# A copy that joins two 16-bit halves: which index runs innermost

## The chip, the cores and the metric

The kernel runs on one core of a Trainium2 chip. A core has a matrix engine (TensorE, PE in the profile, with its weight loads shown apart as PEld), a vector engine (VectorE, DVE), a scalar engine (ScalarE, ACT), GpSimd (POOL), and a queue for data transfers (SyncE, SP). They run beside one another and wait for one another by semaphores. Data lie in SBUF; TensorE writes its results into PSUM, and VectorE and ScalarE read them from there. Both memories have 128 partitions. The metric is the time of the whole program on the device in microseconds, as the median of several runs.

## The reference

Four graph-attention layers run over 16 graphs of 1024 nodes with 256 features. All share one 1024 x 1024 adjacency matrix. Each layer normalises its input and adds its output to it:

```python
h = jnp.maximum(_layernorm(x, axis=-1), 0.0)
x = x + layer(h, adj, W, a)
```

Layers 0, 1 and 3 (with 4, 1 and 4 heads) form `Wh = h @ W`, one score per node as source and one as destination, and mix the values with softmax weights:

```python
e = s_src[:, :, None, :] + s_dst[:, None, :, :]
e = jnp.where(e > 0, e, NEG_SLOPE * e)
alpha = jax.nn.softmax(jnp.where(mask, e, -jnp.inf), axis=2)
h_out = jnp.einsum('bijh,bjhd->bihd', alpha, Wh)
```

Layer 2 has one head, takes its scores from products of queries and keys (`h1 @ h2.T`) and ends in a relu instead of an elu.

## The kernel before, in words

**Tiling.** Rows of x are held in tiles of 128 nodes, eight to a graph (`NT`), and the 256 features in two chunks of 128 (`KC`). Attention works on halves of 512 query nodes.

**Order of work.** Every piece of work of all 64 pairs of graph and layer is a step with an engine, a planned cost and a due time (`Plan.add`). `Plan.order` plays the steps through with the planned costs and fixes one order for each engine; the instructions are then written in that order. Layers of neighbouring graphs overlap, so that TensorE has attention products of one layer while another layer is prepared. On the chip each engine goes through its list in order and waits where something isn't ready. The planned cost of the step that matters here is 0.95 (L920); it steers the order only.

**The prologue of a layer** (`Layer.prologue`, L827) turns normalised rows into values and scores. For each pair of row tiles it does this:
1. ScalarE normalises two tiles into `h` (`normed`, L883).
2. TensorE transposes them (`turned`, L897). A 32-bit transpose is done as two transposes of the two 16-bit halves of each number (`halves`, L587), each written into its own part of one PSUM tile `pp` of shape [128, side 2, chunk 2, 256 nodes] in 16-bit elements. A part holds 512 elements, 1 KB in each partition; the tile is 2 KB.
3. ScalarE copies the PSUM tile to SBUF and joins the halves to 32-bit numbers again (`kept`, L912 to L918). The target is `hTp` for layers 0, 1 and 3, and a slice of `hT` for layer 2. There are four such copies to a layer, 256 in the program.
4. TensorE multiplies the joined tile with the weights (`projected`, L925, by `product`, L569). The joined tile is the stationary operand, so its weight load is the instruction that waits for the copy.
5. ScalarE and VectorE bring the result to `val` and `ke` (L941 to L960).

A second place, `keep` at L1022 to L1024, joins halves in the same manner for the scores of a layer; the change leaves it alone. `pp` has four buffers, `hTp` two and `h` four; a buffer comes free when its last reader is done.

**The rest.** VectorE forms the attention weights `p` (L1089, L1179; L1211 and L1212 for layer 2) and TensorE multiplies them with `val` into `acc` and `accb`. L572 is the line of all of TensorE's products and L585 that of the transposes by halves.

Of the kernel before, what the change touches and what calls it, by code (L numbers as in the profile page):

```python
# [12 lines left out]
U16 = mybir.dt.uint16  # L13
# [516 lines left out]
def fast(  # L530
# [16 lines left out]
    nc = tc.nc  # L547
# [17 lines left out]
    def buf(tag, shape, dtype=F32, name=None):  # L565
        pool = psum if tag in ("pp", "acc", "accb") else sb
        return pool.tile(shape, dtype, name=name or tag, tag=tag, bufs=bufs[tag])

    def product(to, stationary, moving, start, stop):  # L569

        for c in range(0, P, COLS):
            nc.tensor.matmul(  # L572
                to[c : c + COLS],
                stationary[:, c : c + COLS],
                moving,
                start=start,
                stop=stop,
                skip_group_check=True,
            )
# [239 lines left out]
    class Layer:  # L819
# [7 lines left out]
        def prologue(self, due, step, stats, direct=False):  # L827
# [8 lines left out]
            T = {}  # L836
# [3 lines left out]
            for n, its in enumerate(parts):  # L840
# [30 lines left out]
                s = plan.add(DVE, 0.2, at, norm, (*stats[its], ready[-1] if n else None))  # L871
                s = plan.add(POOL, 2.0, at, norm2, (s,))
# [5 lines left out]
            for t0 in range(0, NT, run):  # L878
# [28 lines left out]
                s = plan.add(PE, 0.47 * n, at, turned, norms, take=("pp",) * n, give=("h", "h") * n)  # L907
                turns.update(dict.fromkeys(pairs, s))
            for n, t0 in enumerate(range(0, NT, 2)):
                at, s = due + n * step, turns[t0]  # L910

                def kept(t0=t0):  # L912
                    if self.gat:
                        T["hT", t0] = buf("hTp", [P, KC, 2 * P])
                    else:
                        T["hT", t0] = self.hT[:, :, t0 * P : (t0 + 2) * P]
                    bits = T["hT", t0].bitcast(U16).rearrange("p c (q s) -> p s c q", s=2)
                    nc.scalar.copy(bits, T["tp", t0].bitcast(U16))  # L918

                s = plan.add(ACT, 0.95, at, kept, (s,), take=("hTp",) if self.gat else (), give=("pp",))  # L920
                copies.append(s)
                for k in range(2):
                    t = t0 + k

                    def projected(t=t, t0=t0, k=k):  # L925
                        pv = T["pv", t] = buf("pp", [P, HALF])
                        for c in range(KC):
                            product(
                                pv[:, :cols],
                                T["hT", t0][:, c, k * P : (k + 1) * P],  # L930
                                w[:, c, :cols],
                                start=(c == 0),
                                stop=(c == KC - 1),
                            )

                    s2 = plan.add(
                        PE, 0.9, at + (k + 1) * step / 3, projected, (s, w_ready), take=("pp",),
                        give=("hTp",) if k and self.gat else (),
                    )

                    def evict(t=t):  # L941
                        to = self.val[:, t, :, :d]
                        of = T["pv", t][:, :F].rearrange("p (h d) -> p h d", h=heads)
                        if not self.gat:
                            nc.scalar.copy(to, of)
                            return
                        a = self.val[:, t, :, d : d + 1]

                        nc.scalar.activation(
                            a, T["pv", t][:, F + heads : cols].unsqueeze(2), AF.Exp, scale=1.0 / (SLOPE - 1.0)  # L950
                        )
                        nc.scalar.activation(self.ke[:, :, t], T["pv", t][:, F:cols], AF.Exp)
                        if heads == 1:
                            nc.scalar.mul(to, of, a[:, 0, :])

                    def scaled(t=t):
                        to = self.val[:, t, :, :d]
                        of = T["pv", t][:, :F].rearrange("p (h d) -> p h d", h=heads)
                        a = self.val[:, t, :, d : d + 1]
                        nc.vector.tensor_mul(to, of, a.to_broadcast([P, heads, d]))  # L960

                    many = heads > 1
                    cost = 0.4 if many or not self.gat else 0.8
                    s2 = plan.add(ACT, cost, at, evict, (s2,), give=() if many else ("pp",))
                    if many:
                        s2 = plan.add(DVE, 0.43, at, scaled, (s2,), give=("pp",))
                    evicted.append(s2)
            at = due + 4 * step
            self.ready, self.queries = evicted, ([], [])
            if not self.gat:  # L970
                for dc in range(KC):
                    for n0 in range(0, N, HALF):
# [12 lines left out]
                        s = plan.add(PE, 1.72, at, query, (*copies, *w12_ready), take=("pp",))  # L985
# [8 lines left out]
            if direct:  # L994
                for half in range(2):
                    for hd in range(heads):
# [7 lines left out]
                        def keep(half=half, hd=hd):  # L1004
# [3 lines left out]
                        s = plan.add(  # L1008
                            PE, 0.44, at + (half * heads + hd) * 0.01, spread, tuple(evicted[half * HT : (half + 1) * HT]),
                            take=("pp", f"row{heads}"), wide=True,  # L1010
                        )
# [19 lines left out]
            s = plan.add(PE, 0.14, at, factors, tuple(evicted), take=("pp",))  # L1031
            s = plan.add(ACT, 0.35, at, keep, (s,), give=("pp",))
            s = plan.add(SP, 0.1, at, store, (s,))
            stored = landed(s, at, 16)
            for half in range(2):
                for hd in range(heads):
# [6 lines left out]
                    s = plan.add(SP, 0.5, at + (half * heads + hd) * 0.01, load, (stored,), take=(f"row{heads}",))  # L1043
# [402 lines left out]
```

## Time and profile before

The time before is 3062.7 us (median of 3 runs, 3062.08 to 3062.9). The profiled run's span is 3059.6 us.

| engine | busy us | share |
|---|---|---|
| TensorE, products | 3017.0 | 99% |
| TensorE, weight loads | 2467.5 | 81% |
| VectorE | 2722.5 | 89% |
| ScalarE | 1524.6 | 50% |
| GpSimd | 127.6 | 4% |

How to read it: busy times of different engines overlap, so they don't add up to the span. A row of the profile names the line, the engine, the operation, the tile written and the tiles read, the shape, the count, the busy time with the mean of one instruction in ns, and then the idle time of the engine before these instructions with what ended it. The idle time of an engine that isn't the bottleneck costs nothing by itself. A line of the waits view gives who waited for whom, the sum in us, the number of waits and the longest.

### The profile page before, as it was taken

The numbers are of one execution on the slowest core, as the hardware profiler recorded it, in microseconds if no ns is written. First come the engines' busy times: TensorE is split into PE (matmuls) and PEld (weight loads), VectorE is DVE, ScalarE is ACT, GpSimd is POOL, SyncE is SP. The second block draws the span as 40 slices with busy tenths as digits, with TensorE's granted clock in tenths as the row PEclk, the third lists the DMA queues.
The fourth block names the chain that finished last, engine by engine and source line by source line (L and its number), as shares of the span: only waits on it lengthen the run. The fifth ranks groups of instructions, "written<-read, shape, count | busy, mean of one in ns | idle before, by whom it ended". The sixth has DMA issues, their size and how long they took to land.

```text
span 3059.6 us, 115063 instructions
## 1 busy us (share of the span) xinstructions
PE 3017.0 (99%) x52018; PEld 2467.5 (81%) x52018; DVE 2722.5 (89%) x5551; ACT 1524.6 (50%) x3352; POOL 127.6 (4%) x115
## 2 busy tenths in 40 slices
PE   7999999999999999999999999999999999999998
PEld 5887868778787887878788787887878878786876
DVE  8999969989889898998989989898998989986788
ACT  5573656544644446454454543546444464445443
POOL 1000000000000000000000000000000000000000
PEclk9999999999999999999999999999999999999999
DMA  3110003111010111101111011110111101010110
GB/s 127 51 51 23 27 16 99 37 40 48 20 60 23 37 54 26 58 23 35 49 37 51 19 41 47 37 51 16 55 33 37 55 23 44 23 30 26 30 33 24
DMA packets 82161, 123.41 MB, mean 40 GB/s; under 512 B 6976, under 2 KB 42496, under 8 KB 81664
## 3 DMA queue, kind: packets, MB, share of 16 engines
q1 hardware_dynamic: 81248, 115.47, 12.4%
q8 instruction: 409, 6.70, 0.9%
q14 instruction: 88, 0.72, 0.1%
q10 hardware_dynamic: 416, 0.52, 0.1%
HBM read 98.63 MB, written 17.33 MB: 38 GB/s over the span
## 4 chain that ended last, share of the span: by engine, by line
PE 94%; DVE 4%; ACT 1%; issue 0%; DMA 0%; SPq 0%; DVEq 0%; ACTq 0%
PE pp L572 33%; PE accb L572 29%; PE acc L572 29%; PE pp L585 3%; DVE p L1089 3%; ACT hT L918 0%; ACT hTp L918 0%; DVE bn L813 0%; DVE xt L1066 0%; DMA xt<-in_x_dram 0%; DVE o L1065 0%; DVE mv L814 0%; PE pp L1002 0%; PE tpm L585 0%; PE er L585 0%
## 5 line engine op out<-in xcount | busy, mean ns | idle before, releaser
L1089 DVE SCALAR_TENSOR_TENSOR p<-row,ke,mask 128x512 f32<-128x512 f32 x2048 | 1412.6, 743 | 55.3 <-PE acc L572 51.5
L572 PEld LDWEIGHTS acc<-val,p 128*64 128x64 f32 x32768 | 1066.8, 138 | 80.2 <-issue 37.1
L572 PE MATMUL acc<-val,p 128*64 128x65 f32 x32768 | 1080.9, 223 | 18.2 <-DVE p L1089 17.5
L572 PE MATMUL accb<-val,p 128*64 128x257 f32 x8192 | 928.6, 380 | 0.0
L572 PEld LDWEIGHTS accb<-val,p 128*64 128x64 f32 x8192 | 765.3, 137 | 103.6 <-issue 6.4
L572 PE MATMUL pp<-qT,hT 128*64 128x512 f32 x2048 | 457.7, 592 | 0.0
L572 PE MATMUL pp<-w,hTp 128*64 128x264 f32 (+1 forms) x3072 | 376.9, 386 | 1.3 <-ACT hTp L918 0.3
L572 PEld LDWEIGHTS pp<-qT,hT 128*64 128x64 f32 x2048 | 189.6, 137 | 205.9 <-issue 204.0
L572 PEld LDWEIGHTS pp<-w,hTp 128*64 128x64 f32 x3072 | 241.7, 137 | 81.0 <-ACT hTp L918 8.6
L1246 ACT ACTIVATE o<-accb,rdens 128x256 f32<-128x256 f32 x128 | 60.6, 474 | 470.9 <-DVE rdens L1238 432.9
L886 ACT ACTIVATE h<-xt,nshift,rstd 128x256 f32<-128x256 f32 x512 | 273.4, 600 | 12.7 <-DVE nshift L852 12.7
L918 ACT COPY hTp<-pp 128x1024 uint16<-128x1024 uint16 x192 | 248.8, 1324 | 54.9 <-PE pp L585 54.8
L1211 DVE SCALAR_TENSOR_TENSOR p<-u,p 128x512 f32<-128x512 f32 x256 | 175.6, 686 | 61.9 <-ACT p L1207 61.3
L1206 ACT ACTIVATE u<-pp 128x512 f32<-128x512 f32 x256 | 153.0, 598 | 150.8 <-PE pp L572 136.6
L813 DVE BATCH_NORM_STATS2 bn<-xt 128x6 f32<-128x256 f32 x512 | 212.3, 415 | 14.7 <-DMA xt<-in_x_dram 5.2
L1244 ACT ACTIVATE o<-accb,rden 128x256 f32<-128x256 f32 x128 | 60.6, 473 | 330.5 <-DVE rden L1238 330.5
L849 POOL TENSOR_TENSOR rstd<-rstd,neg_half 128x8 f32<-128x8 f32 (+1 forms) x66 | 117.9, 1786 | 2118.8 <-DVE rstd L846 1799.4
L1212 DVE TENSOR_TENSOR p<-p,mask 128x512 f32<-128x512 f32 x256 | 177.1, 692 | 8.8
L1179 DVE SCALAR_TENSOR_TENSOR p<-row,ke,mask 128x512 f32<-128x512 f32 x256 | 183.4, 739 | 0.0
L1207 ACT ACTIVATE p<-pp,shift_col 128x512 f32<-128x512 f32 x256 | 175.2, 684 | 0.0
L1060 ACT ACTIVATE ex<-o 128x1024 f32<-128x1024 f32 (+1 forms) x195 | 122.1, 626 | 90.2 <-DVE o L1133 85.8
L585 PEld LDWEIGHTS <-h 128*64 128x64 bf16 x4096 | 145.5, 111 | 24.0 <-issue 13.3
(84 smaller groups left out, 1912.4 us busy)
## 6 DMA issues: line engine op xcount, KB each, us to landing
row<-er_d SPq DMA_DIRECT2D x272, 256.0 KB
xt<-in_x_dram SPq DMA_DIRECT2D x32, 512.0 KB
out_dram<-xt SPq DMA_DIRECT2D x31, 512.0 KB
raw<-in_adj_dram SPq DMA_DIRECT2D x4, 1024.0 KB
raw<-in_adj_dram SPq DMA_DIRECT2D x16, 256.0 KB
w<-in_L_gnn_W_dram SPq DMA_DIRECT2D x2, 256.0 KB
wraw<-in_L_gnn_W_dram SPq DMA_DIRECT2D x2, 256.0 KB
er_d<-er_s SPq DMA_DIRECT2D x30, 16.0 KB
```

The costliest lines, as they stand in the source:

```text
L572: nc.tensor.matmul(to[c : c + COLS], stationary[:, c : c + COLS], moving, start=start, stop=stop, skip_group_check=True,)
L585: nc.tensor.transpose(to[c : c + COLS], of[:, c : c + COLS], ident_b)
L813: nc.vector.bn_stats(st, x_tiles[b][:, t, :])
L886: nc.scalar.activation(h, x_tiles[b][:, t, :], AF.Relu, bias=T["shift"][:, t : t + 1], scale=T["rstd"][:, t : t + 1],)
L918: nc.scalar.copy(bits, T["tp", t0].bitcast(U16))
L1060: nc.scalar.activation(ex, o, AF.Exp)
L1089: nc.vector.scalar_tensor_tensor(p, lay.rows[half, hd], lay.ke[:, lay.heads + hd, jt : jt + 1], mask_of(half, jt), op0=OP.max, op1=OP.mult)
L1179: nc.vector.scalar_tensor_tensor(p, lay.rows[half, 0], lay.ke[:, 1, jt : jt + 1], mask_of(half, jt), op0=OP.max, op1=OP.mult)
L1206: nc.scalar.activation(u, e, AF.Exp, scale=1.0 - SLOPE)
L1207: nc.scalar.activation(p, e, AF.Exp, bias=shift_col, scale=SLOPE)
L1211: nc.vector.scalar_tensor_tensor(p, u, 1.0, p, op0=OP.max, op1=OP.mult)
L1212: nc.vector.tensor_mul(p, p, mask_of(half, jt))
```

## The change

The copy runs through 1024 elements in each partition: two chunks c, 256 nodes q and two sides s. In SBUF the two sides of one number are neighbours, in PSUM they lie 512 elements apart. Before, the side is the outermost index: the copy reads PSUM in one contiguous run and writes every second 16-bit place, first all of one side and then all of the other. After it, the side is the innermost index: the copy writes SBUF in one contiguous run (for the slice of `hT`, one run for each chunk) and reads PSUM alternately from the two parts. It is for writing SBUF contiguously. The values, the number of instructions, the planned cost and the steps are the same.

```diff
-                    bits = T["hT", t0].bitcast(U16).rearrange("p c (q s) -> p s c q", s=2)
-                    nc.scalar.copy(bits, T["tp", t0].bitcast(U16))
+                    bits = T["hT", t0].bitcast(U16).rearrange("p c (q s) -> p c q s", s=2)
+                    nc.scalar.copy(bits, T["tp", t0].bitcast(U16).rearrange("p s c q -> p c q s"))
```

## The prediction

> **What bounds the kernel now.** I read the first parts of the page first: engine shares, then the chain that ended last.
>
> ```profile
> PE 3017.0 (99%) x52018; PEld 2467.5 (81%) x52018; DVE 2722.5 (89%) x5551; ACT 1524.6 (50%) x3352; POOL 127.6 (4%) x115
> ...
> PE 94%; DVE 4%; ACT 1%; issue 0%; DMA 0%; SPq 0%; DVEq 0%; ACTq 0%
> ```
>
> TensorE is busy for 99% of the span and is 94% of the chain; ScalarE, the engine of the changed instruction, is busy half of the time and makes 1% of the chain. So what the copy costs ScalarE is not yet a cost of the kernel. It becomes one where TensorE stands still for the copy. The order of all instructions is fixed when the program is built, from planned costs that the change leaves alone, so TensorE can't do other work instead: a wait there is lost for good, and a wait removed there is won.
>
> Next, the changed line and who waits for it, and TensorE's list of waits.
>
> ```profile
> L918 ACT COPY hTp<-pp x192: 1296/1321/1371, 14.5 to 2991.0; 128x1024 uint16<-128x1024 uint16 x192
> L918 ACT COPY hT<-pp x64: 1296/1331/1358, 174.2 to 2881.0; 128x1024 uint16<-128x1024 uint16 x64
> ...
>   PEld pp L572: 12.3, 55
>   PE pp L572: 0.3, 1
> ```
>
> ```profile
> PEld acc L572 <- DVE p L1089: 15.9, 18, 4.7
> ...
> PEld pp L572 <- ACT hTp L918: 8.6, 35, 0.6
> ...
> PEld pp L572 <- ACT hT L918: 3.7, 20, 0.2
> ```
>
> There are 192 + 64 = 256 copies of 1.32 us. TensorE stood still for 56 of them, 12.3 + 0.3 = 12.6 us in all, or 0.4% of the span. That is the ceiling of what a faster copy can win directly. One such wait, from the timeline:
>
> ```profile
> 717.10 1.11 PE L585 MATMUL pp<-ident_b,h 128*64 128x128 bf16 x32
> 717.81 2.50 ACT L918 COPY hTp<-pp 128x1024 uint16<-128x1024 uint16 x2 [0.34 <-PE pp L585]
> 717.94 0.68 PEld L572 LDWEIGHTS pp<-w2v,hT 128*64 128x64 f32 x8
> 719.17 0.86 PEld L572 LDWEIGHTS pp<-w,hTp 128*64 128x64 f32 x10 [0.56 <-ACT hTp L918]
> ```
>
> The transposes end, the copy starts at 717.81 and takes 1.32 us to 719.12, TensorE runs one other projection and then stands until 719.17, 50 ns after the copy. Here each ns on the copy is a ns on the kernel.
>
> How many copies are like this? I followed each of the 256 copies in the trace to the first weight load that reads its tile. The distance from the copy's end to that load is under 0.06 us for 66 copies, under 0.3 us for 99, under 0.6 us for 147 and under 1.0 us for 170; the other 86 have more. About 0.05 us is the handover itself. So the slack is short: the median is under 0.5 us.
>
> **What a copy element costs.** The rows by shape show what the loop order could change.
>
> ```profile
> L988 ACT COPY qT<-pp 128x512 f32<-128x512 f32 x64 | 37.6, 587 | 114.4 <-PE pp L572 114.4
> L945 ACT COPY val<-pp 128x256 f32<-128x256 f32 x128 | 44.7, 378 | 70.1 <-PE pp L572 69.9
> L1024 ACT COPY er_s<-er 32x256 uint16<-32x256 uint16 x30 | 13.2, 439 | 14.3 <-PE er L585 14.3
> L741 ACT COPY mask<-tpm 128x512 bf16<-128x512 bf16 x8 | 4.4, 607 | 0.0
> L952 ACT ACTIVATE ke<-pp 128x8 f32<-128x8 f32 x256 | 45.8, 186 | 0.0
> L952 ACT ACTIVATE ke<-pp 128x2 f32<-128x2 f32 x128 | 22.5, 176 | 0.0
> ```
>
> Contiguous copies from PSUM take 587 ns for 512 and 378 for 256 elements: (587 - 378)/256 = 0.82 ns an element, so 1024 would take 587 + 512 x 0.82 = 1007 ns. L918 takes 1324, that is 317 ns or 0.31 ns an element more. L1024 writes in the same stepped way and also pays: 439 - 378 = 61 ns, 0.24 an element. L741 moves 16-bit data contiguously on both sides at 607, next to the 587 of fp32. So the surcharge belongs to the write with a step of two 16-bit places, not to 16-bit data.
>
> **What the Trainium skill says.** "ScalarE: Activation LUTs", section "What ACT_TABLE_LOAD costs": 186 ns + 0.833 ns an element for immediate scale and bias; 1024 give 1039 (estimate). The trace agrees roughly for contiguous copies (612 priced, 587 measured at 512), and not for L918. "Advanced Engine Details and Errata", "PSUM Cachelines": PSUM has lines of 8 bytes and "every two consecutive elements should be contiguous for best throughput". No row of this trace reads PSUM with many hops, so it neither confirms nor denies it. "Vector Engine (DVE) Microarchitecture Reference", "Measured stream behaviour on trn2": on the other vector engine and in SBUF, a source that hops at every element costs about 0.65 cycle an element more, though one stream alternating between two regions ran at full rate in one measurement. Both halves bear on this change; no run here shows either.
>
> **The change part by part.** The instruction count, waits, semaphores, buffers and transposes stay. Only the walk of 256 copies changes.
> - Removed: the stepped write. All 1024 elements now go to adjacent 16-bit places. By L741 this is worth the whole surcharge, 0.31 us a copy, 256 x 0.31 = 79 us of ScalarE's time, nearly all of it beside other work.
> - Added: the read alternates between the two halves of the PSUM tile, 1 KB apart; each element lies in another line than the one before. Lower bound: free, and the copy takes 1.01 to 1.04 us. Middle: a hop costs as much as an element, 1007 + 1024 x 0.82 = 1847 ns, or 186 + 1024 x 1.67 = 1.89 by the skill's price doubled. Upper: two more places in the element's time, 1007 + 2 x 840 = 2.69 us. The 0.65 cycle of VectorE would give 1007 + 1024 x 0.54 = 1.56 us.
>
> Rows of few elements are all there is to choose by. L952 writes with a step of 32 bytes: from 2 to 8 elements it takes 186 - 176 = 10 ns more, 1.7 ns an element, twice the 0.82 of a contiguous copy. The reciprocals of VectorE read PSUM: 164 ns for one element, 173 for four that lie 65 words apart, 3 ns an element instead of about 1. These differences are near the scatter of the rows, but both say that a hop to another line isn't free, on a write and on a PSUM read. I take **1.87 us**, +0.55 us a copy.
>
> What of that lands on TensorE: for each copy, the extra less its slack (distance minus 0.05), never below zero. Summed over the 256: 23 us for +0.27 (100 copies), 57 us for +0.55 (147 copies), 130 us for +1.0 (172 copies). Copies that follow one another directly (66 do) hand part of the delay on; counting twice the extra for the second of each pair, less what the first has already held TensorE up, gives 58 instead of 57. TensorE's waits don't earn the time back, as each pair of transposes and projection has its own wait in the fixed order. Behind the copy on ScalarE are the next pair's normalisation, the val/ke evictions and the exponentials of another layer; with 50% of idle time they catch up within a few us. VectorE has 11% idle and gains some as TensorE slows. 3062.7 + 57 = **3120 us**.
>
> **Rivals.**
> 1. *Alternation is free* (faster): 1.01 to 1.04 us, 0.3 us less. 66 copies have a wait to give back, 12.6 us by the waits view; most single waits are about 0.2 us, shorter than 0.3, so 10 to 12 us come back: 3051. For it: the full-rate measurement of two alternating regions, and that each 8-byte line is used four times before it is left. Against it: no second line is shown to be held open, and the rows with hops above.
> 2. *Mild*: VectorE's 0.65 cycle, 1.56 us, +0.24 to 0.27: 23 us by the sum above, 3086.
> 3. *A draw*: the read pays as much as the write paid; copies 1.25 to 1.4 us, 3056 to 3068.
> 4. *Heavy*: over 2.1 us; at 2.3 (+1.0) 130 us, 3193; ScalarE would hold 256 us more, 58%, still not the bound.
>
> **How the numbers follow.** Middle 0.42, free 0.33, heavy 0.09, mild 0.10, draw 0.06. The forecast is the middle's, 3120. The range runs from 3047, so that the free case is inside, to 3152, where a copy of 2.0 us (+0.7, about 80 us) ends; the heavy case is left out above. Faster by over 0.2% (6 us): 0.33. Within: 0.06. Slower: 0.10 + 0.42 + 0.09 = 0.61.
>
> **What would show it right or wrong.** L918's mean decides between the cases: 1.85 to 1.95 us as forecast, about 1.02 if the alternation is free, and no change in any other row. In the waits of TensorE, those for L918 should grow from 12.6 us towards 65 to 70, from 56 to some 150 waits, while the wait for p (L1089) at start and end stays. ScalarE's busy time should go from 1524.6 to about 1665. I would be wrong on size, with the copy as forecast, if other waits overlapped those of the copy: TensorE slowed gives VectorE time, so that waits for p vanish, but these are only 33 us and lie in the first and last 60 us. I would be wrong in kind if reading two halves is served at full rate; then the waits for L918 fall to almost nothing and the kernel ends near 3051.

## The result and the profile after

The changed kernel takes 3049.0 us (median of 4 runs, 3047.99 to 3051.08), the one before beside it 3062.39: a ratio of 0.9958 with a 95% interval of 0.9941 to 0.9975. It is 13.4 us faster (by the interval 7.7 to 18), where the forecast was 57 us slower. The first rival, a free alternation at 3051 us, is what happened. The page's engine shares first:

```profile
PE 3009.3 (99%) x52018; PEld 2508.5 (82%) x52018; DVE 2719.1 (89%) x5551; ACT 1461.6 (48%) x3352; POOL 127.6 (4%) x115
```

ScalarE is busy 63 us less, TensorE's products 8 us and VectorE 3 us less. The weight loads are busy 41 us more, though a single one takes as long as before (a mean of 136 ns in both): their records overlap less, for a reason that no run here shows. The changed line, with minimum, median and maximum of one instruction in ns, and below it who waited for it (us, number of waits):

```profile
L918 ACT COPY hTp<-pp x192: 988/1012/1043, 14.6 to 2980.5; 128x1024 uint16<-128x1024 uint16 x192
L918 ACT COPY hT<-pp x64: 989/1012/1059, 175.1 to 2871.3; 128x1024 uint16<-128x1024 uint16 x64
...
  PEld pp L572: 0.6, 2
```

A copy takes 1.012 us instead of 1.324, and TensorE waits for it twice instead of 56 times, 0.6 us instead of 12.6. The other waits of TensorE are where they were:

```profile
PEld acc L572 <- DVE p L1089: 15.7, 19, 4.7
...
PEld L585 <- DVE pos L728: 14.1, 2, 13.0
...
PEld pp L572 <- ACT hTp L918: 0.6, 2, 0.3
```

The profiled spans differ by 3059.6 - 3049.3 = 10.3 us, the medians by 13.4; the 12.0 us of vanished waits lie between. (The profiled execution of the changed kernel was the slowest of its four.) The order of the instructions is the same in both kernels. Only the access patterns of 256 of them differ.

### The profile page after: what moved, and what is told of

Read it like the earlier page. It is cut to its first block, busy times and chain, and to the rows that moved or that the text cites. A ratio compares the mean times of both kernels' runs of the same rounds, so it can differ in the third digit from the quotient of the medians.

```text
span 3049.3 us, 115063 instructions
## 1 busy us (share of the span) xinstructions
PE 3009.3 (99%) x52018; PEld 2508.5 (82%) x52018; DVE 2719.1 (89%) x5551; ACT 1461.6 (48%) x3352; POOL 127.6 (4%) x115
## 3 DMA queue, kind: packets, MB, share of 16 engines
q1 hardware_dynamic: 81248, 115.47, 12.6%
## 4 chain that ended last, share of the span: by engine, by line
PE 95%; DVE 4%; issue 0%; DMA 0%; ACT 0%; SPq 0%; DVEq 0%
PE pp L572 33%; PE acc L572 30%; PE accb L572 29%; PE pp L585 4%; DVE p L1089 2%; DVE bn L813 0%; DVE xt L1066 0%; DMA xt<-in_x_dram 0%; DVE o L1065 0%; DVE mv L814 0%; PE pp L1002 0%; PE tpm L585 0%; PE er L585 0%; DVE rden L1122 0%; DVE parts L1308 0%
## 5 line engine op out<-in xcount | busy, mean ns | idle before, releaser
L572 PEld LDWEIGHTS acc<-val,p 128*64 128x64 f32 x32768 | 1078.5, 139 | 71.5 <-issue 37.0
L572 PEld LDWEIGHTS pp<-w,hTp 128*64 128x64 f32 x3072 | 267.6, 137 | 53.9 <-issue 7.7
L918 ACT COPY hTp<-pp 128x1024 uint16<-128x1024 uint16 x192 | 190.4, 1011 | 58.2 <-PE pp L585 56.9
L585 PEld LDWEIGHTS <-h 128*64 128x64 bf16 x4096 | 149.4, 111 | 21.3 <-issue 13.4
```

Source lines behind the costliest of these rows:

```text
L572: nc.tensor.matmul(to[c : c + COLS], stationary[:, c : c + COLS], moving, start=start, stop=stop, skip_group_check=True,)
L585: nc.tensor.transpose(to[c : c + COLS], of[:, c : c + COLS], ident_b)
L918: nc.scalar.copy(bits, T["tp", t0].bitcast(U16).rearrange("p s c q -> p c q s"))
```

## The experiments

### A part of the copies at a time

```diff
+                    if self.gat:
+                        bits = T["hT", t0].bitcast(U16).rearrange("p c (q s) -> p c q s", s=2)
+                        nc.scalar.copy(bits, T["tp", t0].bitcast(U16).rearrange("p s c q -> p c q s"))
+                    else:
                         bits = T["hT", t0].bitcast(U16).rearrange("p c (q s) -> p s c q", s=2)
                         nc.scalar.copy(bits, T["tp", t0].bitcast(U16))
```

This is the first of the two; the second has `if not self.gat`.

> The 192 copies into hTp take the new loop order, the 64 into hT keep the old one. Theory A (the copy is 0.31 us shorter and only TensorE's waits for it come back): copies 1.01 us into hTp and 1.33 into hT; the 8.6 + 0.3 us of waits for hTp vanish, those for hT (3.7 us) stay; 3062.4 - 9 = 3053 us. Theory B (the gain is in how SBUF and PSUM are accessed beside TensorE, not in the wait): the gain goes with the number of copies, 192/256 of 13.4 = 10.0, 3052.3 us; the two theories are close here and told apart by the next runs.

> The 64 copies into hT take the new order, the 192 into hTp the old one. Theory A: 3.7 us of waits for hT vanish, 3058.7 us. Theory B: 64/256 of 13.4 = 3.4 us, 3059.0. With the run before: the two parts should add up to the whole (13.4 us) if neither hides the other.

Measured: the 192 copies into hTp alone give 3053.83 us (ratio 0.9976, 0.9967 to 0.9984), 7.8 us less than the 3061.67 of before; the 64 into hT alone 3056.51 (0.9983, 0.9976 to 0.9989), 5.2 us less. The sum is 13.0, next to the 13.4 of the whole, so it seems that neither hides the other. In the first run the waits for hTp are at 0.6 us and those for hT stay at 3.7:

```profile
PEld pp L572 <- ACT hT L922: 3.7, 20, 0.2
...
PEld pp L572 <- ACT hTp L919: 0.6, 2, 0.3
```

Here L919 is the new form and L922 the old one. In the second it is the other way round (8.4 us of waits for hTp are left). A quarter of the copies gives more than a quarter of the gain, as theory A has it by the waits, but the intervals don't separate the theories: 5.2 us, by the interval 3.4 to 7.3, against 3.7 and 3.4.

### The copy's time put back, with the new access order

```diff
+                    nc.scalar.copy(T["hT", t0].bitcast(U16)[:, 0, : 2 * P], T["tp", t0].bitcast(U16)[:, 0, 0, :])
                     nc.scalar.copy(bits, T["tp", t0].bitcast(U16).rearrange("p s c q -> p c q s"))
```

> The changed kernel with one more ScalarE copy of 256 16-bit elements from the same PSUM tile ahead of each joining copy, overwritten by it. Together they take about 1.01 + 0.28 = 1.30 us, nearly the 1.32 of the kernel before, with the new access order. Theory A: the waits are back, about 12 us, and the time is 3059 to 3062. Theory B: the time stays near 3049 to 3052.

Measured: 3074.9 us, ratio 1.0042 (1.0029 to 1.0056). It lies above even theory A's 3062. The reason is in the pair: the second copy starts 32 ns after the first one's end, where other neighbours on ScalarE overlap by about 100 ns. The trace records a wait for ScalarE's own semaphore with each of these 256 second copies, so it is most likely the program that holds the second back until the first is done. The pair takes 373 + 32 + 1012 = 1417 ns, 0.09 us more than the old copy and not slightly less. The waits of TensorE are back, and larger (L919 is the joining copy):

```profile
PEld pp L572 <- ACT hTp L919: 17.1, 51, 0.7
...
PEld pp L572 <- ACT hT L919: 5.9, 20, 0.3
```

Theory B, that the access order itself helps TensorE, falls: with the new order and a copy that ends late the kernel is slow. What counts is when the copy ends. A run below says the same from the other side, with the old order in a fast kernel.

### The time that was forecast for the copy

```diff
+                    nc.scalar.copy(T["hT", t0].bitcast(U16), T["tp", t0].bitcast(U16).rearrange("p s c q -> p s (c q)"))
                     nc.scalar.copy(bits, T["tp", t0].bitcast(U16).rearrange("p s c q -> p c q s"))
```

> The changed kernel with a contiguous copy of all 1024 16-bit elements ahead of each joining copy, overwritten by it: together about 1.01 + 0.92 = 1.93 us, near the 1.87 that was forecast for the copy. Theory A with the forecast's slack sum: +0.61 us over the copy before is worth about 65 us, so 3120 to 3132. If delays are absorbed (the sum counts waits that overlap): under 3100. If they pile up behind ScalarE: over 3145.

Measured: 3186.81 us, ratio 1.041 (1.0396 to 1.0424), 125 us more than before. The pair takes 1012 + 32 + 1012 = 2.06 us, +0.73 instead of the +0.61 expected. The forecast's slack sum, done again for +0.73, gives 84 us over 157 copies: the number of waits is right (154 for L919 in the list of weight loads), the sum is a third too low. That list holds nearly all of the loss (L917 is the first copy of a pair):

```profile
PEld pp L572 <- ACT hTp L919: 91.1, 128, 2.5
...
PEld pp L572 <- ACT hT L919: 21.6, 26, 1.0
PEld pp L572 <- ACT hT L917: 18.9, 23, 0.8
```

These are 131.6 us, 119 more than the 12.3 of before. The timeline shows one way in which a wait grows longer than the copy's extra (start, length, engine; in brackets the engine's idle time before and its releaser):

```profile
739.08 1.01 ACT L919 COPY hT<-pp 128x1024 uint16<-128x1024 uint16 x1
...
740.13 1.01 ACT L917 COPY hT<-pp 128x1024 uint16<-128x1024 uint16 x1
740.17 1.11 PE L585 MATMUL pp<-ident_b,h 128*64 128x128 bf16 x32
...
741.17 1.01 ACT L919 COPY hT<-pp 128x1024 uint16<-128x1024 uint16 x1
742.08 1.02 ACT L917 COPY hTp<-pp 128x1024 uint16<-128x1024 uint16 x1
743.13 1.01 ACT L919 COPY hTp<-pp 128x1024 uint16<-128x1024 uint16 x1
...
744.04 1.02 ACT L917 COPY hTp<-pp 128x1024 uint16<-128x1024 uint16 x1
744.19 0.27 PEld L572 LDWEIGHTS pp<-w,hTp 128*64 128x64 f32 x4 [2.50 <-ACT hTp L919]
744.19 0.69 PE L572 MATMUL pp<-w,hTp 128*64 128x264 f32 x2 [2.04 <-ACT hTp L919]
```

The transposes of 740.17 end at 741.28, but ScalarE still has a pair for hT to finish; the pair for hTp starts at 742.08 and ends at 744.14, and TensorE stands for 2.04 us. Over all 256, a copy starts about 0.6 us after its transposes ended in the kernel before and the pair 1.0 us here. Adding that later start to each copy's extra raises the sum from 84 to more than 140 us, and the measured 125 lies between. For the short pad the same sums are about 7 and 12 to 13 us, measured 13.2. So the later start accounts for what the sum lacked in size; no run changes it alone.

### What an access pattern costs by itself

This kernel leaves the whole computation out. It has six ScalarE copies of 1024 elements in a row for each pattern, for instance these two, and two patterns on VectorE:

```python
nc.scalar.copy(one.rearrange("p (a s) -> p a s", s=2), h.rearrange("p (s a) -> p a s", s=2))   # L1425
nc.scalar.copy(one.rearrange("p (b a) -> p b a", b=32), h.rearrange("p (a b) -> p b a", b=32)) # L1429
```

> Leaves the whole computation out and writes copied data: it only times ScalarE copies of 1024 elements a partition, six in a row of each access pattern, and two of VectorE. Theory A1 (ScalarE reads PSUM at full rate however it hops, and only narrow stepped writes pay): contiguous, alternating and all scattered 16-bit and fp32 reads 1.01 us; 16-bit writes with step 2 1.32, with wider steps more. Theory A2 (two places at a time stay open, so that alternating is free but a fresh line at each element is not): alternating 1.01, reads with steps of 8, 64 and 256 bytes 1.5 us or more. Alternating read with stepped write isn't possible for the same data; the write step alone with one half gives the write's share.

The groups by shape (busy us, mean ns of one):

```profile
L1423 ACT COPY dst<-src 128x1024 uint16<-128x1024 uint16 x6 | 28.1, 4682 | 0.2
L1421 ACT COPY dst<-src 128x1024 uint16<-128x1024 uint16 x6 | 14.5, 2420 | 0.2
L1442 ACT COPY dst<-big 128x1024 f32<-128x1024 f32 x6 | 11.9, 1987 | 0.2
L1435 ACT COPY dst<-xs 128x1024 uint16<-128x1024 uint16 x6 | 11.4, 1901 | 0.2
...
L1419 ACT COPY dst<-src 128x1024 uint16<-128x1024 uint16 x6 | 7.7, 1291 | 0.2
...
L1450 DVE COPY dst<-big 128x1024 f32<-128x1024 f32 x6 | 7.3, 1224 | 0.2
L1433 ACT COPY dst<-xs 128x1024 uint16<-128x1024 uint16 x6 | 6.9, 1157 | 0.2
...
L1415 ACT COPY dst<-src 128x1024 uint16<-128x1024 uint16 x6 | 6.1, 1012 | 1.6 <-POOL dst L1406 1.4
L1425 ACT COPY dst<-src 128x1024 uint16<-128x1024 uint16 x6 | 6.1, 1012 | 0.2
...
L1429 ACT COPY dst<-src 128x1024 uint16<-128x1024 uint16 x6 | 6.1, 1012 | 0.2
```

What each line is, and its mean:

| copy by ScalarE, 1024 elements | ns |
|---|---|
| 16-bit or fp32, contiguous on both sides (L1415, L1438) | 1012 |
| 16-bit, PSUM read alternating between two halves, the new order (L1425) | 1012 |
| 16-bit, PSUM read with steps of 8, 64, 256 bytes (L1427, L1429, L1431) | 1012 |
| fp32, PSUM read with steps of 8 and 64 bytes (L1444, L1446) | 1012 |
| 16-bit, write with a step of 4 bytes, the old order (L1419) | 1291 |
| 16-bit, write with steps of 8 and 16 bytes (L1421, L1423) | 2420, 4682 |
| fp32, write with steps of 8 and 32 bytes (L1440, L1442) | 1055, 1987 |
| 16-bit, SBUF read alternating, and with a step of 64 bytes (L1433, L1435) | 1157, 1901 |

VectorE's fp32 copies from PSUM take 1224 ns, contiguous (L1448) as with a read step of 64 bytes (L1450). Theory A1 holds for PSUM: ScalarE reads it at the contiguous rate in every pattern tried, so no pair of open lines (A2) is needed. The old order's surcharge is the stepped 16-bit write: its read is contiguous, and one pass that writes every second place, without the second side, costs the same (L1417, 1292 ns). A pattern measured in a quiet kernel could differ beside TensorE's writes; in the changed kernel it is 1012 too.

### The planned cost instead of the copy

```diff
-                s = plan.add(ACT, 0.95, at, kept, (s,), take=("hTp",) if self.gat else (), give=("pp",))
+                s = plan.add(ACT, 1.24, at, kept, (s,), take=("hTp",) if self.gat else (), give=("pp",))
```

> The kernel before with the planned cost of the copy set to 1.24 (its measured 1.32 less the overlap with its neighbour) instead of 0.95; the order of work changes on all engines. If the waits for the copy come from a plan that thought the copy shorter than it was, they fall from 12.6 us to a few and the time goes to about 3052, as with the change. If the plan has no better place for them, or the tuned due times fit the old cost, the time is equal or higher: 3062 to 3075.

Measured: 3051.79 us, ratio 0.9967 (0.9955 to 0.9979), with the old copies of 1.33 us. The copy's own view, with who waited for it:

```profile
L918 ACT COPY hTp<-pp x192: 1291/1327/1374, 14.5 to 2980.5; 128x1024 uint16<-128x1024 uint16 x192
...
  PEld pp L572: 0.7, 3
```

Three waits of 0.7 us in all are left of 56 with 12.6. So the waits came from a plan that held the copy to be shorter than it was. The copy is as long as ever; what changed is the order in which the engines do their work. A number in the plan wins 10.0 us, most of what the faster copy wins. And since these copies have the old access order, a kernel can be fast without the new one: theory B falls here too. Only this one value was tried with the old copy, so how closely the plan must fit isn't shown, and this run alone doesn't rule out a lucky order. The long pad below, where the same correction wins 127 us, speaks against luck.

The same number together with the new copy:

> The changed kernel with the planned cost 1.24: the order of work that took the waits away from the kernel before, now with copies of 1.01 us. Theory A (both ways remove the same waits): nothing is left to win, 3047 to 3053. Rival (the shorter copy and the other order remove different waits): the gains add up, 3038 to 3043.

Measured: 3050.86 us (0.9963, 0.9949 to 0.9976). The gains don't add up; both remove the same 12 us. The planned cost at the new copy's own value, 0.92:

> The changed kernel with the planned cost 0.92, the copy's measured 1.01 less the overlap with its neighbour. Only the order changes. Expected 3046 to 3056: the copy's waits are down to 0.6 us already, so what moves is the luck of another order with due times tuned for the old one.

Measured: 3050.38 us (0.9961, 0.9947 to 0.9975), no difference from the change that can be told.

And the long pad with a plan that knows of it (the same edit, 1.95):

> The kernel with the second full copy ahead of each joining copy (2.06 us a pair, 3187 us) with the planned cost of the step set to 1.95. If the 125 us lost there are waits of a plan that doesn't know of the longer copy, most come back: 3060 to 3090. If ScalarE or the buffers (two hTp, four pp) set the limit, it stays over 3130.

Measured: 3059.57 us, ratio 0.9992 (0.9983 to 1.0), from 3187. The waits for the joining copy, 91.1 and 21.6 us with the old plan, are these with the new one:

```profile
PEld pp L572 <- ACT hTp L919: 7.1, 16, 1.9
PEld pp L572 <- ACT hT L919: 4.6, 3, 3.2
```

It came out a hair below its expected 3060 to 3090. The 125 us that 0.73 us more in 256 copies had cost against the kernel before are all won back by the order of work, though about 10 us are left against the changed kernel. Neither ScalarE (56% busy) nor the buffers were the limit.

### The other joining copy

```diff
-                nc.scalar.copy(er_s.bitcast(U16).rearrange("n (q s) -> n s q", s=2), T["er"][:n].bitcast(U16))
+                bits = er_s.bitcast(U16).rearrange("n (q s) -> n q s", s=2)
+                nc.scalar.copy(bits, T["er"][:n].bitcast(U16).rearrange("n s q -> n q s"))
```

> The changed kernel with the same loop order also in the joining copy of the scores (L1024, 46 instructions of 0.44 us). Theory A: they get 61 to 70 ns shorter, no TensorE instruction waits for them (their result goes through DRAM to rows needed some 10 us later), so 3049 within 2 us. Rival: the rows arrive earlier and waits of VectorE for them fall, 3046 or less.

Measured: 3050.13 us (0.9961, 0.9947 to 0.9974), no different from the change alone. The 46 copies take 360 ns instead of 439, a saving of 79 where 61 to 70 were expected, and no engine is seen to wait for them. No version tried beats the changed kernel.

## Why the prediction was wrong

- *What bounds the kernel*: right. TensorE is the bound, the ceiling of a direct gain is the 12.6 us of waits for the copy, and 12.0 us of them are gone.
- *Removed, the stepped write, 0.31 us a copy*: right within 5 ns: 317 worked out, 1324 - 1012 = 312 measured. The contiguous value worked out from two other rows, 1007, was measured at 1012.
- *Added, the alternating read, "I take 1.87 us"*: this is the step that failed. The forecast put +0.86 us on the read (1.87 against the contiguous 1.007), and it costs nothing: 1.012 us, as for a contiguous copy. I had three kinds of evidence. L952 was a stepped write, and its 1.7 ns an element is what such fp32 writes cost: (1987 - 190)/1024 = 1.75, with 190 ns as a small instruction's fixed part, estimated from L952's 176 to 186. But a write's price says nothing about a read. The reciprocals' 9 ns between one and four elements from PSUM are hardly a hop's price, since VectorE's copy reads with a step of 64 bytes at the contiguous rate; the reciprocals' own step of 65 words wasn't tried, and what the 9 ns are stays open. And the Trainium skill's "PSUM Cachelines" in "Advanced Engine Details and Errata" names matmuls alone as what is slowed; its "every two consecutive elements should be contiguous" doesn't show in any PSUM read of ScalarE or VectorE here. The full-rate alternation of "Measured stream behaviour on trn2" in "Vector Engine (DVE) Microarchitecture Reference", to which I gave less weight, pointed the right way, in part by luck: it is about VectorE and SBUF, and ScalarE's alternating read from SBUF takes 1157 ns here, where the nearest contiguous row from SBUF, L1061 of the kernel before, takes 1060.
- *+0.55 us is worth 57 us*: not tested at that value, but the same sum gave 84 where 125 were measured at +0.73, so it was too low by a third. The term missing, as far as the sums above show, is the later start of a copy behind other copies; that ScalarE's other work would "catch up within a few us" was wrong for copies in a row.
- *The first rival's 10 to 12 us*: 13.4 by the medians with an interval of 7.7 to 18, 10.3 in the profiled runs. Its 66 copies with a wait to give back are 56 by the waits view. That the forecast's range reached down to 3047 is owed to this rival, not to the mechanism that the forecast chose.
- *The order is fixed, so a wait is lost for good*: right for this change, and half of the story. The waits existed because the plan's 0.95 wasn't the copy's 1.24.

## What to carry to other kernels

Price a read and a write, PSUM and SBUF separately; if the trace has no row for the access in question, a row of another kind is no stand-in. Time that access by itself first, as the small kernel above does in a few lines, or say that between a free read and a dear one the point forecast is little more than a guess. When an engine with a fixed order waits for an instruction that is off the bottleneck, compare the plan's cost with the measured duration first: here one number was worth 10.0 us, and the faster instruction 13.4. To estimate what a longer instruction costs, count its own queue too, not only the slack behind it.

## What the runs showed of the hardware

- ScalarE copies 1024 elements from PSUM in 1012 ns in each read pattern tried: contiguous, 2-byte elements alternating 1 KB apart, and steps of 8, 64 and 256 bytes. From SBUF the pattern counts: 1157 alternating, 1901 with a step of 64 bytes. The small kernel has no contiguous read from SBUF beside them; L1061 of the kernel before, an activation over 1024 fp32 elements from SBUF, takes 1060.
- Stepped writes by ScalarE cost by step, and 16-bit ones more than fp32 ones: 1291, 2420 and 4682 ns at 4, 8 and 16 bytes, against 1055 and 1987 at 8 and 32 bytes for fp32.
- In both pads the second copy of a pair starts 31 to 32 ns after the end of the first, where the joining copies that follow one another in the changed kernel mostly overlap by about 100 ns. In 27 places of the run with the long pad a copy into another slice of `hT`, which overwrites nothing, has the same gap behind a joining copy. All of these copies have a wait for ScalarE's own semaphore. So the gap goes with a wait in the program rather than with the overwriting; no run leaves the wait out.
